# Moving the copy of the scan's last column for two of four channel groups from ScalarE to VectorE, in a state-space network on one core

## The chip, the cores and the metric

The kernel runs on one core of a Trainium2 chip. The metric is the device time in microseconds. Before the change the median of three runs is 6207.15 us (6202.91 to 6214.02).

The core's engines work side by side, each on its own queue in order: TensorE (PE in the profile; PEld is its weight load), VectorE (DVE), ScalarE (ACT), GpSimd (POOL), and SyncE (SP), which only issues DMAs here. An instruction waits on semaphores for what others have to finish first; all behind it on the same engine wait with it.

## What is computed

Input x is 8 images of 384 channels and 32 x 32 pixels. Four layers follow one another, each a group norm, a block, and a residual sum. Layers 0 and 2 are Mamba blocks, and they hold the part that matters here, a recurrence along the 1024 pixels of an image:

```python
def step(h, inp):
    dA_t, dBu_t, C_t = inp          # exp(dt*A), dt*u*B, C
    hst = dA_t * hst + dBu_t
    return (hst, jnp.einsum('bdn,bn->bd', hst, C_t))
```

There are 768 inner channels d with 16 states n each, so 12,288 independent recurrences for each image. Layer 1 is a 1x1 convolution, a filter in the frequency domain of 8 x 8 patches, a 3 x 3 depthwise convolution and a gate; layer 2 has an MLP behind its Mamba block; layer 3 is a 3 x 3 depthwise convolution.

## The kernel before

**Tiling.** An image is cut into two halves of T = 512 pixels (NCH = 2). A half of a layer-0 or layer-2 image is a *chunk*: 2 layers x 8 images x 2 halves = 32 chunks. A chunk has NQ = 24 *steps*; a step is 4 groups (j = 0 to 3) of 128 recurrences (8 channels x 16 states), so 768 steps in all. The chunk's number in its image is `s["c"]`: 0 for the first half, 1 for the second.

**A step t**, with the function that writes each part:

- `begins`: a DMA brings dt*u, repeated over the states, into the SBUF tile `g` (128 x 4 x 512, AHEAD + 1 = 5 buffers).
- `times`: GpSimd multiplies all of g by B (one instruction, 128 x 2048).
- `decays`: TensorE writes dt for each group into its PSUM bank `dA{j}`; the four banks are used by every step.
- `exps`: ScalarE turns each bank into exp(dt*A).
- `scans`: VectorE runs the recurrence of each group as one scan instruction of 512 columns. SHARE is 2 everywhere, so `low` is 2: the scans of groups 0 and 1 write into g (SBUF), those of groups 2 and 3 into their banks (PSUM). Then VectorE multiplies groups 2 and 3 by C, from the banks into g.
- `carries`: in a first half (`s["c"] == 0`) the last column of each scan is kept in the SBUF tile `carry`, since the second half starts from it (line 847). ScalarE does it before the change: one copy of 128 x 2 for groups 0 and 1 together (line 868) and one of 128 x 1 for each bank (line 873). A second half has no such copies.
- `states`: GpSimd multiplies groups 0 and 1 by C, in place in g (one instruction, 128 x 1024). In place means that the last columns must have been copied before: the condition is `carried(t, 0)` (line 886).
- `gathers`: TensorE sums the 16 states of all four groups into `y`, `gatings`: VectorE multiplies y by the gate z.

**Side jobs.** `front` prepares the next chunk (projections, a short convolution, softplus, three-part bf16 copies of dt), `finish` projects the chunk before, and `layer1`, `mlp` and `layer3` run between the steps, all on the same engines.

**Order.** Nothing is scheduled on the chip: each engine executes its list in order. The lists are written ahead by a planner in the kernel, `Order`, which runs the generators above as processes. Each process yields the engine that it wants and a condition; `Clocks.op` keeps an estimate of when each engine is free and each piece of data is known, by prices of its own (a VectorE instruction: 0.075 us plus 0.00104 a column; a GpSimd instruction: 0.14 plus 0.00212 a column). The planner always lets that process go on which can begin first. GpSimd's list is therefore an alternation of `times` for a later step and `states` for an earlier one, with the side jobs' instructions between. TensorE may overwrite a bank for the next step when it has been read (line 816 to 818; for groups 2 and 3 that includes the carry).

All engine calls go through one helper, so nearly every instruction of the profile stands at L189; they are told apart by the tiles that they write and read.

Of the kernel before, what the change touches and what calls it, by code (L numbers as in the profile page):

```python
# [11 lines left out]
AF = mybir.ActivationFunctionType  # L12
# [13 lines left out]
T = 512  # L26
NCH = L // T
# [222 lines left out]
def tile_conv_preact_d4(ctx: ExitStack, tc: tile.TileContext, a: dict, out: bass.AP):  # L250
# [10 lines left out]
    clocks = Clocks()  # L261
    order = Order(clocks)
    tensor = Timed(nc.tensor, clocks, "PE")
    vector = Timed(nc.vector, clocks, "DVE")
# [18 lines left out]
    def on(engine, *aps, when=None, due=None, next_=False):  # L283


        def ready():
            t = when() if when else 0.0
            return None if t is None else max(t, clocks.known(*aps) if aps else 0.0)

        return engine, ready, due, next_  # L290
# [8 lines left out]
    class Tokens:  # L299
# [5 lines left out]
        def when(self):  # L305
            return min(self.free) if self.free else None
# [62 lines left out]
    def exp_set():  # L369
        nc.scalar.preload_act_table_set(SET_EXP)  # L370
        clocks.free["ACT"] += 1.28
        act_set["now"] = "exp"

    def act(out_, in_, func, **kw):
        if func in (AF.Exp, AF.Ln):
            if act_set["now"] != "exp":
                exp_set()
        elif func not in (AF.Identity, AF.Copy, AF.Square, AF.Abs):
            if act_set["now"] != func:
                clocks.free["ACT"] += 1.28  # L380
            act_set["now"] = func
        scalar.activation(out_, in_, func, **kw)
# [28 lines left out]
    carry = const.tile([P, 4 * NQ], F32, name="carry")  # L411
# [355 lines left out]
    said = {}  # L767

    def seen(*keys):


        def ready():
            return None if any(k not in said for k in keys) else 0.0

        return ready
# [57 lines left out]
    def scans():  # L833
        for t, (s, i) in enumerate(steps):
            for j in range(4):
                yield on("DVE", dAs[j], when=lambda: (
                    None if ("exp", t, j) not in said or ("times", t) not in said
                    else clocks.known(s["g", i][:, j, :])
                ))
                g = s["g", i]  # L840
                low = 4 - SHARE[i % NSUB]
                q = 4 * i + j
                vector.tensor_tensor_scan(
                    g[:, j, :] if j < low else dAs[j],
                    dAs[j],
                    g[:, j, :],
                    0.0 if s["c"] == 0 else carry[:, q : q + 1],
                    ALU.mult,
                    ALU.add,
                )  # L850
                ahead["scans"] += 1
                said["scan", t, j] = True
            for j in range(low, 4):
                yield on("DVE", dAs[j])
                vector.tensor_mul(g[:, j, :], dAs[j], s["bc"][:, 1, :])
                said["product", t, j] = True
            start_jobs(t + 1)

    def carries():
        for t, (s, i) in enumerate(steps):  # L860
            if s["c"] == NCH - 1:
                continue
            low = 4 - SHARE[i % NSUB]
            yield on("ACT", when=lambda: (
                None if ("scan", t, low - 1) not in said else clocks.known(s["g", i][:, 0:low, :])
            ))
            g = s["g", i]
            act(carry[:, 4 * i : 4 * i + low].unsqueeze(2), g[:, 0:low, T - 1 : T], AF.Copy)
            said["carry", t, 0] = True
            for j in range(low, 4):  # L870
                q = 4 * i + j
                yield on("ACT", dAs[j], when=seen(("scan", t, j)))
                act(carry[:, q : q + 1], dAs[j][:, T - 1 : T], AF.Copy)
                said["carry", t, j] = True
# [470 lines left out]
    def start_jobs(t):  # L1345
        n, i = divmod(t, NQ)
        if i or n >= len(chunks):
            return
        s = chunks[n]
        order.add(gates(s, 1), t + 8)  # L1350
        if s["c"] == 0 and n + NCH < len(chunks):
            m = chunks[n + NCH]
            order.add(measured(m), t + NQ + 4)
        if n + 1 < len(chunks):
            later = chunks[n + 1]
            order.add(front(later), t + NQ - 26)
            order.add(gates(later, 0), t + NQ - 4)
        order.add(finish(s), t + NQ + 10)
# [28 lines left out]
    for name, gen in (  # L1387
        ("begins", begins), ("times", times), ("decays", decays), ("exps", exps),
        ("scans", scans), ("carries", carries), ("states", states), ("gathers", gathers), ("gatings", gatings),
    ):  # L1390
        p = procs[name] = {
            "gen": gen(), "due": 0, "ready": 0.0, "done": None, "first": ("PE", "ACT", "SP"),
        }
        order.processes.append(p)
        order.advance(p)
# [141 lines left out]
```

## Time and profile before

| | |
|---|---|
| median of three runs | 6207.15 us |
| the profiled execution | 6204.07 us |
| its span, first to last instruction | 6202.2 us |
| granted TensorE clock, mean | 0.973 |
| ScalarE, carry<-g, 128x2 | x384, 205 ns mean, 78.8 us |
| ScalarE, carry<-dA, 128x1 | x768, 174 ns mean, 133.4 us |
| GpSimd, `times` (128x2048) | x768, 4535 ns mean, 3479.6 us |
| GpSimd, `states` (128x1024) | x768, 2359 ns mean, 1810.9 us |
| VectorE, scans without and with a carry | 1209 to 1212 and 1269 to 1271 ns |
| VectorE, product with C (128x512, one operand in PSUM) | x1536, 677 ns mean |
| VectorE, COPY | x1 (gain<-ps_gain, 128x384 out of PSUM) |

How to read it: the profile groups instructions by the tiles that they write and read (`carry<-g` writes carry and reads g), gives their number, the busy time, the mean duration, and the idle time of the engine right before them with what ended it. A share of busy time is an average over chunks of four kinds (first and second halves, layer 0 and layer 2), so a view of one chunk tells more. A chunk of 24 steps takes 169 to 199 us between 1506 and 4928 us.

### The profile page before, as it was taken

What the parts mean: (1) busy time and instruction counts of PE and PEld (TensorE: products, weight loads), DVE (VectorE), ACT (ScalarE), POOL (GpSimd) and SP (SyncE); (2) the same over time, 40 slices, a digit from 0 to 9 for tenths busy, and PEclk for the clock granted to TensorE, in tenths of its full rate; (3) what the DMA queues carried; (4) which work ended last, traced back from release to release, by engine and by line L of the source; (5) the groups of instructions that cost most, each with busy time, mean ns of one, the idle gap of its engine ahead of it and who ended that gap; (6) DMA issues with size and microseconds to landing.
All of it is one profiled execution on the core that took longest, in us unless ns stands there. A gap on an engine that the chain in (4) does not pass through costs nothing.

```text
span 6202.2 us, 62614 instructions
## 1 busy us (share of the span) xinstructions
PE 5799.2 (94%) x19022; PEld 2184.1 (35%) x19022; DVE 5616.8 (91%) x6381; ACT 4241.3 (68%) x7942; POOL 5725.3 (92%) x2028
## 2 busy tenths in 40 slices
PE   6878999999999999999989999999999999999998
PEld 2223333333333333333333333333333333333333
DVE  5999999999998999998887899899998999989994
ACT  5656677677667767776676676777767777677753
POOL 4999999999999999989997999999999999999991
PEclk8889999999999999999999999999999999999999
DMA  6877878877887888787777888878888788888871
GB/s 178 193 184 186 195 190 194 204 188 193 190 193 185 196 205 189 192 205 186 180 185 183 199 196 219 200 198 209 198 215 201 200 207 198 212 205 197 207 197 58
DMA packets 346724, 1195.88 MB, mean 193 GB/s; under 512 B 40516, under 2 KB 142580, under 8 KB 248084
## 3 DMA queue, kind: packets, MB, share of 16 engines
q1 hardware_dynamic: 346388, 1191.88, 79.1%
q8 instruction: 152, 2.49, 0.2%
q14 instruction: 184, 1.51, 0.1%
HBM read 1040.73 MB, written 150.99 MB: 192 GB/s over the span
## 4 chain that ended last, share of the span: by engine, by line
DVE 25%; PE 13%; POOL 8%; DMA 4%; issue 4%; ACT 4%; SPq 0%; POOLq 0%; DVEq 0%; ACTq 0%
DVE g L189 11%; DVE dA L189 8%; POOL g L189 6%; DVE u L189 2%; PE ps_dn L189 2%; PE ps_up L189 2%; PE ps_dw L189 2%; PE y L189 2%; PE dA L189 2%; DMA g<-dud 2%; DVE ps_dw L189 1%; PE ps_z L189 1%; DMA dts<-dtd 1%; PE ps_out L189 1%; DVE st L189 1%
## 5 line engine op out<-in xcount | busy, mean ns | idle before, releaser
L189 POOL TENSOR_TENSOR g<-g,bc 128x1024 f32<-128x1024 f32 (+1 forms) x1536 | 5243.4, 3447 | 248.1 <-ACT carry L189 94.1
L189 ACT ACTIVATE dA<-dA,w_A 128x512 f32<-128x512 f32 x3072 | 2018.6, 661 | 931.0 <-PE dA L189 919.4
L189 PE MATMUL dA<-dts,selr 96*128 96x512 bf16 x3072 | 1190.0, 390 | 233.2 <-DVE g L189 207.6
L189 DVE TENSOR_TENSOR_SCAN g<-dA,carry,g 128x512 f32<-128x512 f32 x768 | 955.4, 1269 | 75.1 <-POOL g L189 61.1
L189 DVE TENSOR_TENSOR g<-dA,bc 128x512 f32<-128x512 f32 x1536 | 994.5, 677 | 17.3 <-ACT carry L189 16.4
L189 DVE TENSOR_TENSOR_SCAN g<-dA,g 128x512 f32<-128x512 f32 x768 | 909.4, 1209 | 85.7 <-POOL g L189 77.8
L189 DVE TENSOR_TENSOR_SCAN dA<-dA,carry,g 128x512 f32<-128x512 f32 x768 | 952.2, 1271 | 28.0 <-ACT dA L189 27.4
L189 DVE TENSOR_TENSOR_SCAN dA<-dA,g 128x512 f32<-128x512 f32 x768 | 909.0, 1212 | 62.3 <-ACT dA L189 61.7
L189 PE MATMUL y<-g,sely 128*32 128x512 f32 x6144 | 857.0, 627 | 38.0 <-POOL g L189 35.6
L189 PEld LDWEIGHTS <-selr 96*128 96x128 bf16 x3072 | 300.2, 98 | 1113.0 <-issue 1072.0
L189 PE MATMUL ps_in<-xf,w_in 128*128 128x512 f32 x1152 | 562.7, 610 | 10.0 <-ACT xf L189 7.6
L189 PE MATMUL ps_z<-xf,w_z 128*128 128x512 f32 x1152 | 567.8, 597 | 3.6 <-DVE dt L189 3.6
L189 PE MATMUL ps_up<-t,mw 128*128 128x512 f32 x1152 | 556.0, 596 | 7.1 <-DVE u L189 5.2
L189 PE MATMUL ps_out<-u,w_out 128*128 128x512 f32 x1152 | 547.5, 594 | 0.4 <-ACT carry L189 0.4
L189 PE MATMUL ps_dn<-h,mw 128*128 128x512 f32 x1152 | 545.3, 594 | 1.6 <-ACT h L189 1.6
L189 PE MATMUL ps_dw<-tp,diag 128*128 128x512 f32 x864 | 438.8, 609 | 9.6 <-ACT diag L189 9.6
L189 PEld LDWEIGHTS y<-g,sely 128*32 128x32 f32 x6144 | 126.3, 109 | 599.2 <-issue 313.0
L189 PEld LDWEIGHTS ps_in<-xf,w_in 128*128 128x128 f32 x1152 | 218.6, 195 | 263.8 <-issue 234.2
L189 POOL TENSOR_TENSOR dt<-dt,u 128x512 f32<-128x512 f32 x192 | 244.3, 1274 | 72.4 <-PE ps_dr L189 56.3
L189 PEld LDWEIGHTS ps_dn<-h,mw 128*128 128x128 f32 x1152 | 217.8, 190 | 259.9 <-issue 235.3
L189 PEld LDWEIGHTS ps_up<-t,mw 128*128 128x128 f32 x1152 | 214.4, 190 | 267.2 <-issue 230.4
L189 PEld LDWEIGHTS ps_z<-xf,w_z 128*128 128x128 f32 x1152 | 215.9, 191 | 252.7 <-issue 215.2
(118 smaller groups left out, 6451.1 us busy)
## 6 DMA issues: line engine op xcount, KB each, us to landing
g<-dud SPq DMA_DIRECT2D x768, 1024.0 KB, 8.2
dtd<-pc SPq DMA_DIRECT2D x192, 384.0 KB, 4.0
dts<-dtd SPq DMA_DIRECT2D x192, 384.0 KB, 7.8
mw<-in_l_mlp_w SPq DMA_DIRECT2D x192, 384.0 KB, 6.5
dud<-dt SPq DMA_DIRECT2D x768, 64.0 KB, 3.2
xf<-in_x SPq DMA_DIRECT2D x16, 768.0 KB, 9.1
x<-in_x SPq DMA_DIRECT2D x16, 768.0 KB, 11.9
x_mid<-x SPq DMA_DIRECT2D x16, 768.0 KB, 7.0
```

The source lines that it names most:

```text
L189: return call(out_, *args, **kw)
```

## The change

VectorE copies the last columns of groups 0 and 1 itself, in one instruction that stands right behind the scan of group 1 and ahead of the scan of group 2. It is no process of its own: it is written in the same turn of `scans` as that scan. ScalarE keeps the copies of the two banks. The condition of `states`, `carried(t, 0)`, is the same and is now met by VectorE.

```diff
@@ scans
                 ahead["scans"] += 1
                 said["scan", t, j] = True
+                if j == low - 1 and s["c"] < NCH - 1:
+                    vector.tensor_copy(
+                        carry[:, 4 * i : 4 * i + low].unsqueeze(2), g[:, 0:low, T - 1 : T]
+                    )
+                    said["carry", t, 0] = True
             for j in range(low, 4):
@@ carries
             low = 4 - SHARE[i % NSUB]
-            yield on("ACT", when=lambda: (
-                None if ("scan", t, low - 1) not in said else clocks.known(s["g", i][:, 0:low, :])
-            ))
-            g = s["g", i]
-            act(carry[:, 4 * i : 4 * i + low].unsqueeze(2), g[:, 0:low, T - 1 : T], AF.Copy)
-            said["carry", t, 0] = True
             for j in range(low, 4):
```

## The prediction

> **What bounds the kernel now.** I read the page's shares first, then the busy time of the engines in four stretches, one chunk of 24 steps each: a first half and a second half of a layer-0 image, then the same of a layer-2 image.
>
> ```profile
> PE 5799.2 (94%) x19022; PEld 2184.1 (35%) x19022; DVE 5616.8 (91%) x6381; ACT 4241.3 (68%) x7942; POOL 5725.3 (92%) x2028
> ```
> ```profile
> 1506.00:1696.00 190.00, 172.70 (x604) 65.47 (x603) 173.25 (x205) 137.20 (x297) 176.82 (x63) 0.96 0.79 190
> 1696.00:1865.00 169.00, 164.20 (x560) 61.78 (x558) 164.65 (x181) 116.21 (x211) 168.34 (x54) 1.00 0.82 196
> 4542.00:4729.00 187.00, 182.72 (x599) 69.19 (x599) 175.21 (x202) 137.40 (x267) 182.32 (x71) 1.00 0.86 206
> 4729.00:4928.00 199.00, 193.41 (x618) 73.20 (x617) 187.88 (x213) 137.78 (x220) 187.21 (x68) 1.00 0.82 202
> ```
>
> Columns of the second view: stretch, its length, then PE, weight loads, DVE, ACT, POOL, clock, DMA share, GB/s. Only first halves carry anything over, so only they change. There a step takes 190/24 = 7.92 us in layer 0 with VectorE busy 7.22 and GpSimd 7.37, and 7.79 us in layer 2 with VectorE 7.30, GpSimd 7.60 and TensorE 7.61. No engine has 0.8 us to spare except ScalarE (5.7 of 7.9). In a second half of layer 0, without carries, GpSimd is busy 168.3 of 169 us. So VectorE and GpSimd are both near their limit, and the gap between 7.92 and 7.37 is what waits cost. One of these waits is the change's target:
>
> ```profile
> POOL g L189 <- ACT carry L189: 94.1, 54, 7.1
> ```
>
> 54 waits, 94.1 us: GpSimd may not overwrite g with the C product before ScalarE has copied the last column of g, and ScalarE comes to that copy late.
>
> **The change, part by part.**
>
> (a) Removed: 384 ScalarE copies (16 first halves x 24 steps) of 128x2.
>
> ```profile
> L189 ACT ACTIVATE carry<-g 128x2 f32<-128x2 f32 x384 | 78.8, 205 | 43.9 <-DVE g L189 29.7 <-issue 8.3 <-POOL g L189 2.5
> ```
>
> 384 x 0.205 = 79 us less on an engine that is busy 68%. Nothing on the path follows its busy time, so I cost this at nothing by itself. What may follow is the 94.1 us above. Late next would be the scan itself: "POOL g <- DVE g" already stands at 60.2 us. The upper bound of the gain is 94 us.
>
> (b) Added: 384 VectorE copies of 128x2 from SBUF to SBUF, each right behind the scan that wrote its second column. VectorE has no such row. Its smallest: the 128x96 TENSOR_SCALAR at 24.80 us took 0.12 from its start to the next start, and BATCH_NORM_AGGREGATE 0.225 start to start. A dependent pair costs more than an independent one: in layer 2 the gating (u from y) starts 0.034 us behind the end of the instruction that writes its y (96 times), while independent neighbours overlap by 0.084. That is 0.12 us for the wait on the scan. So a copy costs between 0.12 (no bubble) and 0.35 (bubble and the dearer row); I take 0.12 + 0.12 = 0.24, since a copy resembles the plain elementwise row more than the aggregate. 384 x 0.24 = 92 us on VectorE, of which its idle time in first halves (0.65 us a step) could hide most.
>
> (c) The wait that the copy may bring. VectorE's instructions here are nearly all of a kind: one operand in PSUM, one in SBUF. The only plain one-source elementwise instruction from SBUF to SBUF is the scaling of w_A, and there are two of it:
>
> ```profile
> 24.80 0.20 DVE L189 TENSOR_SCALAR w_A<-w_A 128x96 f32<-128x96 f32 x1
> 24.92 0.75 DVE L189 SCALAR_TENSOR_TENSOR u<-ps_in,w_vec,u 128x510 f32<-128x510 f32 x1
> ```
> ```profile
> 2787.11 0.95 DVE L189 TENSOR_SCALAR w_A<-w_A 128x96 f32<-128x96 f32 x1
> 2787.98 1.28 DVE L189 TENSOR_TENSOR_SCAN dA<-dA,carry,g 128x512 f32<-128x512 f32 x1
> ```
> ```profile
> 2783.49 4.51 POOL L189 TENSOR_TENSOR g<-g,bc 128x2048 f32<-128x2048 f32 x1
> ```
>
> The columns are start, duration, engine. At 24.8 us GpSimd runs nothing and the instruction takes 0.20 us. At 2787 the same instruction takes 0.95, and it ends at 2788.06, 0.06 behind the end of GpSimd's 4.51 us product (2783.49 + 4.51 = 2788.00). I read this as VectorE held until GpSimd's running instruction is done. Against it stands a one-source SBUF row that is not stretched, BATCH_NORM_STATS2 (676 ns mean over 96 calls), so not every such instruction is held; the copy resembles the scaling more than the statistics.
>
> [...]
>
> What would the hold cost? I took the end of the second scan in each of the 384 first-half steps and looked at what GpSimd was running. In 332 of them it was inside an instruction, mostly the 4.5 us one. One such step:
>
> ```profile
> 1624.76 2.33 DVE L189 TENSOR_TENSOR_SCAN g<-dA,g 128x512 f32<-128x512 f32 x2
> 1627.00 2.32 DVE L189 TENSOR_TENSOR_SCAN dA<-dA,g 128x512 f32<-128x512 f32 x2
> ```
> ```profile
> 1626.16 4.52 POOL L189 TENSOR_TENSOR g<-g,bc 128x2048 f32<-128x2048 f32 x1 [1.58 <-DMA g<-dud]
> ```
>
> Now the second pair of scans starts at 1627.00. With the copy ahead of them they would wait until GpSimd is done at 1630.68, 3.6 us later. Summed over the 384 steps the rest of GpSimd's instruction is 711 us, 1.85 a step. Queued behind the copy on VectorE are the two scans in PSUM, both products, the next step's scans, and the convolutions and sums of the side jobs; exps, PSUM banks, TensorE's next decays and GpSimd's next C product wait for these.
>
> 711 us will not all show. Once VectorE is late, GpSimd runs out of work at the C product of that step (it needs the scan and the copy), stands idle, and the copy passes at once. The hold thus turns two loosely coupled queues into two that meet once a step, at the end of a GpSimd instruction. A step then takes about the longer of VectorE's work from copy to copy and GpSimd's work from C product to C product. I added both up per first-half step in the trace (all but the first chunk, which is start-up), with 0.24 us for the copy, and averaged the larger of the two: 8.22 us in layer 0 against 7.91 now, 8.49 in layer 2 against 7.82. That is 0.31 x 192 + 0.67 x 192 = 60 + 129 = 188 us. Busy times hold no waits, so the removed 94 us is already inside this difference. The order is written anew by the planner, which knows no hold; a more even alternation would lower the sum, waits on TensorE and DMAs would raise it.
>
> (d) Nothing else moves: no DMA, no semaphore on SP, and TensorE's condition for the next decays asks only for the copies from the two banks, which stay.
>
> **Sum.** 6204.07 us (the profiled execution: span 6202.2 and 1.9 around it; 0.05% under the median of 6207.15) + 188 = 6392, say 6390, 3.0% slower.
>
> **Rivals.**
> 1. *No hold, the change does what its words suggest* (the other side). For it: the statistics row, and that 2 elements are very few. Against it: the 0.95 us row. Then GpSimd gets back its 94 us and VectorE gives 92, about half of it hidden: 6204 - 94 + 46 = 6156, with ends at 6110 (all hidden) and 6202 (none hidden). It decides from the point where a copy takes under about 0.5 us with GpSimd busy.
> 2. *The hold in full.* VectorE does not settle behind GpSimd but asks at any moment, as now: 711 + 92, less its present idle time of 0.65 x 384 = 250, gives 553: 6757. For it: 270 of the 332 cases fall into the 4.5 us instruction, and VectorE is as busy as GpSimd. Against it: GpSimd then idles ahead of each C product and lets the copy through.
> 3. *The hold is there but hidden.* VectorE settles so that nearly every copy finds GpSimd waiting for it; only (a) and (b) are left, 6204 - 94 + 92 = 6202. In the trace only 52 of 384 moments are like that.
>
> **How the numbers follow.** Forecast 0.55, rival 1 0.20, rival 2 0.15, rival 3 0.10. Changes under 0.2% can't be told from none. Rival 1 gives 0.16 faster, 0.03 same, 0.01 slower; rival 3 gives 0.02, 0.06, 0.02; forecast and rival 2 are slower. So 0.18, 0.09, 0.73. The forecast alone spans 6270 to 6550 (half and nearly twice its sum). For 8 in 10 the range takes in rival 3, the upper half of rival 1 and the lower part of rival 2: 6150 to 6650.
>
> **What would show it.** A row of VectorE copies, x384: a mean of 1 to 2 us, ending with GpSimd's instructions, shows the hold; 0.1 to 0.3 us refutes it. ScalarE's carry<-g row and GpSimd's waits on ACT carry for g should go in every case. First halves should go from 7.8-7.9 to 8.2-8.5 us a step, second halves stay at 7.05 and 8.3; GpSimd's idle time should end on VectorE. If copies are long but steps are not, rival 3 holds; a copy mean near 1.9 and steps over 9 us mean rival 2. The prediction is wrong if two elements do not count as that kind of instruction.

## The result, and the profile after

| | before | after |
|---|---|---|
| median of all runs | 6207.89 us (6202.91 to 6214.02, 4 runs) | 6510.57 us (6507.76 to 6520.41, 4 runs) |
| profiled execution | 6204.07 us | 6512.05 us |
| its span | 6202.2 us | 6510.2 us |

The ratio is 1.0492, with a 95% interval of 1.0479 to 1.0505: slower by 4.9%. The forecast was slower by 3.0% (6390 us), the range 6150 to 6650.

The shares of the profile after, to be set beside those of before:

```profile
PE 5886.7 (90%) x19022; PEld 2212.6 (34%) x19022; DVE 6015.9 (92%) x6765; ACT 4196.9 (64%) x7558; POOL 5732.6 (88%) x2028
```

VectorE has 384 instructions and 399 us of busy time more. GpSimd has the same work (5733 against 5725 us) and a smaller share: it waits more. Where the 399 us are, and for what GpSimd waits, two groups tell (columns as on the page: busy us, mean ns, idle time ahead and what ended it):

```profile
L189 DVE COPY carry<-g 128x2 f32<-128x2 f32 x384 | 402.2, 1047 | 13.1
L189 POOL TENSOR_TENSOR g<-g,bc 128x1024 f32<-128x1024 f32 x768 | 1807.8, 2355 | 350.6 <-DVE carry L189 267.8 <-DVE g L189 71.6 <-DMA g<-dud 2.1
```

A copy of two columns takes 1047 ns on average, nearly as long as a scan of 512 (1205 ns). GpSimd's C product, which waited 94 us for ScalarE's copy, now waits 268 us for VectorE's. The stretches of the first halves (chunks 8 and 24, the same as shown of before, and the second half behind each):

```profile
1567.00:1767.00 200.00, 172.17 (x591) 65.78 (x590) 192.60 (x228) 131.51 (x270) 180.39 (x64) 0.96 0.77 183
1767.00:1938.00 171.00, 165.15 (x563) 61.14 (x563) 165.89 (x184) 120.55 (x215) 167.97 (x53) 1.00 0.80 191
4732.00:4943.00 211.00, 189.67 (x600) 71.04 (x600) 206.62 (x225) 133.96 (x242) 184.85 (x73) 0.98 0.77 191
4943.00:5143.00 200.00, 189.18 (x604) 70.95 (x604) 189.43 (x215) 135.61 (x216) 192.96 (x68) 0.97 0.81 197
```

The first halves went from 190 to 200 and from 187 to 211 us, the second halves from 169 to 171 and from 199 to 200. Over all chunks the first halves hold 304 of the 308 us that the span grew by.

How a copy comes to be long is best seen in a row of steps of chunk 24, VectorE first, then GpSimd (start, duration, and in brackets the idle time ahead; a row of x2 or x3 is a run of instructions and shows the shape of its first alone):

```profile
4803.62 4.35 DVE L189 COPY carry<-g 128x2 f32<-128x2 f32 x1
...
4818.69 0.17 DVE L189 COPY carry<-g 128x2 f32<-128x2 f32 x1
...
4826.47 3.87 DVE L189 COPY carry<-g 128x2 f32<-128x2 f32 x1
```
```profile
4801.11 6.83 POOL L189 TENSOR_TENSOR g<-g,bc 128x1024 f32<-128x1024 f32 x2
4808.11 6.82 POOL L189 TENSOR_TENSOR g<-g,bc 128x1024 f32<-128x1024 f32 x2 [0.17 <-DVE carry L189]
4819.00 11.31 POOL L189 TENSOR_TENSOR g<-g,bc 128x1024 f32<-128x1024 f32 x3 [4.08 <-DVE carry L189]
4830.49 6.83 POOL L189 TENSOR_TENSOR g<-g,bc 128x1024 f32<-128x1024 f32 x2 [0.17 <-DVE carry L189]
```

The first copy starts at 4803.62 and ends at 4807.97; GpSimd's pair of products ends at 4801.11 + 6.83 = 4807.94. The third ends at 4830.34, GpSimd's three at 4819.00 + 11.31 = 4830.31. Between them stands a copy of 0.17 us: GpSimd was idle (4.08 us) and waited for it. So either VectorE waits for GpSimd or GpSimd for VectorE, about once a step. Of the 384 copies 219 took over 0.4 us, and 210 of those ended 0.024 to 0.030 us behind the end of a GpSimd instruction; 196 of the 219 began within a 128x2048 one. Behind 137 of the other 165 GpSimd had been waiting for the copy (over 0.15 us), which leaves 28 steps in which neither waited.

### The profile page after: what moved, and what is told of

It reads as the page before. It is cut to its first block, busy times and chain, and to the rows that moved or that the text cites. A ratio compares the mean times of both kernels' runs of the same rounds, so it can differ in the third digit from the quotient of the medians.

```text
span 6510.2 us, 62617 instructions
## 1 busy us (share of the span) xinstructions
PE 5886.7 (90%) x19022; PEld 2212.6 (34%) x19022; DVE 6015.9 (92%) x6765; ACT 4196.9 (64%) x7558; POOL 5732.6 (88%) x2028
## 4 chain that ended last, share of the span: by engine, by line
DVE 37%; PE 17%; ACT 9%; POOL 7%; issue 5%; DMA 2%; SPq 0%; DVEq 0%; POOLq 0%; ACTq 0%
DVE g L189 15%; DVE dA L189 11%; POOL g L189 5%; DVE carry L189 3%; PE ps_dw L189 3%; DVE u L189 3%; PE y L189 3%; PE ps_up L189 2%; PE dA L189 2%; PE ps_dn L189 2%; ACT dA L189 2%; PE ps_z L189 1%; ACT L189 1%; ACT L370 1%; DMA g<-dud 1%
## 5 line engine op out<-in xcount | busy, mean ns | idle before, releaser
L189 POOL TENSOR_TENSOR g<-g,bc 128x2048 f32<-128x2048 f32 (+1 forms) x1536 | 5247.8, 3443 | 436.4 <-DVE carry L189 269.2
L189 PE MATMUL dA<-dts,selr 96*128 96x512 bf16 x3072 | 1205.4, 395 | 404.3 <-DVE g L189 383.5
L189 DVE TENSOR_TENSOR_SCAN g<-dA,g 128x512 f32<-128x512 f32 x768 | 905.1, 1205 | 50.4 <-POOL g L189 36.6
L189 PE MATMUL y<-g,sely 128*32 128x512 f32 x6144 | 874.8, 635 | 32.4 <-POOL g L189 31.4
L189 PE MATMUL ps_dn<-h,mw 128*128 128x512 f32 x1152 | 563.6, 610 | 7.1 <-ACT z L189 5.0
L189 ACT ACTIVATE carry<-dA 128x1 f32<-128x1 f32 x768 | 132.0, 173 | 454.8 <-DVE dA L189 437.3
L189 DVE COPY carry<-g 128x2 f32<-128x2 f32 x384 | 402.2, 1047 | 13.1
```

What stands on the lines that cost most here:

```text
L189: return call(out_, *args, **kw)
```

## The experiments

My theory: VectorE's copy of two SBUF columns to SBUF waits until GpSimd's running instruction ends, as the 210 copies that end 0.024 to 0.030 us behind one do, and a copy of one column does not. Rival A: the loss comes from the place of the copy and the order that the planner made with it. Rival B: any SBUF to SBUF copy, or any copy of two elements, is held. Twelve kernels were run. "Held" is a row over 0.4 us. The diffs show the lines of the step; the declarations of extra tiles are left out.

**Two copies of one column** (`e1_two_singles`). The planner is told the price of the single copy, so each engine's order is that of the changed kernel.

```diff
-                    vector.tensor_copy(
-                        carry[:, 4 * i : 4 * i + low].unsqueeze(2), g[:, 0:low, T - 1 : T]
+                    clocks.op(
+                        "DVE", "tensor_copy", carry[:, 4 * i : 4 * i + low].unsqueeze(2),
+                        [g[:, 0:low, T - 1 : T]],
                     )
+                    for k in range(low):
+                        nc.vector.tensor_copy(
+                            carry[:, 4 * i + k : 4 * i + k + 1], g[:, k, T - 1 : T]
+                        )
```

> The 128x2 copy is cut into two copies of 128x1 at the same place; every engine's order is that of the changed kernel. [...] Rival A (the time comes from where the copy stands and from the order the planner made of it, not from a hold): 6500 to 6560 us, since place and order are the same and one more instruction is added. Rival B (any SBUF to SBUF copy on VectorE is held): at least 6500 us, with rows up to 4.5 us.

Measured: 6231.02 us, ratio to before 1.0044 (1.0030 to 1.0058). None of the 768 copies is held, the longest takes 0.157 us.

```profile
L859 DVE COPY carry<-g 128x1 f32<-128x1 f32 x768 | 104.0, 141 | 0.0
```

Twice the instructions and a quarter of the time. Rival A falls, and with it the first half of rival B: 280 us of the loss go, with the place and the order unchanged.

**The same two columns by a reduction** (`e2_reduce`).

```diff
-                    vector.tensor_copy(
-                        carry[:, 4 * i : 4 * i + low].unsqueeze(2), g[:, 0:low, T - 1 : T]
+                    vector.reduce_max(
+                        carry[:, 4 * i : 4 * i + low], g[:, 0:low, T - 1 : T], axis=mybir.AxisListType.X
                     )
```

> The copy is written as a maximum over one element (a reduction of 128x2x1 to 128x2): the same data, count, place and order as in the changed kernel, another operation. Theory (the hold belongs to copies and their like, as the batch-norm statistics row suggests it is not every one-source SBUF instruction): rows of 0.1 to 0.3 us, 6150 to 6220 us. Rival A (place and order): 6500 to 6530. Rival B (any one-source SBUF to SBUF instruction of two elements is held): 6500 to 6530, rows up to 4.5 us.

Measured: 6225.02 us, ratio 1.0036 (1.0023 to 1.0049).

```profile
L189 DVE TENSOR_REDUCE carry<-g 128x2 f32<-128x2 f32 x384 | 59.6, 155 | 13.2
```
```profile
POOL g L189 <- DVE carry L189: 123.4, 72, 5.6
```

The first line is VectorE's group, the second GpSimd's wait (total, times, longest). This is the cleanest pair of the study: one operation swapped, all else the same, 6511 - 6225 = 286 us. TensorE's granted clock, 0.973 before and 0.959 after, is 0.970 here, so its fall went with the hold; no run sets the clock alone. The run also shows what rival 1 had wrong: without any hold the change is still no gain, but 0.36% slower. The 94 us that GpSimd waited for ScalarE became 123 us that it waits for VectorE. I had expected up to 6220 here, and it came out a little above.

**A copy that nobody needs** (`e3_dummy_pair` and `e4_dummy_single`). The kernel before, ScalarE's copies left in, and an unused copy between constant tiles added; in the second run one column, in the same order. The planner's order is not that of the kernel before.

```diff
+                if j == low - 1 and s["c"] < NCH - 1:
+                    clocks.op("DVE", "tensor_copy", spare2, [vec2[:, 0:2]])
+                    nc.vector.tensor_copy(spare2[:, 0:2], vec2[:, 0:2])
```

> The kernel before, with ScalarE's carry copies left as they are, and a copy of 128x2 from one constant SBUF tile to an unread one added behind the second scan of each first-half step. Nothing waits for it but what stands behind it on VectorE. Theory (hold): 384 copies of about 1 to 1.8 us mean, 6207 plus 150 to 450 = 6360 to 6660 us. Rival A (the loss comes from the carry's dependency on VectorE and GpSimd's wait for it): 6207 plus 0 to 60, copies of 0.1 to 0.3 us.

> The same with a copy of 128x1 in place of 128x2; every engine's order is that of the run with the 128x2 copy. Theory: no hold, copies of 0.1 to 0.2 us, 6207 plus 0 to 60 us. Rival B (any SBUF copy is held): as the 128x2 copy, within 1%.

Measured: 6602.46 us (1.0642, 1.0628 to 1.0657) with two columns, 6258.12 us (1.0086, 1.0073 to 1.0100) with one. VectorE's groups of the two runs:

```profile
L856 DVE COPY spare<-vec 128x2 f32<-128x2 f32 x384 | 453.2, 1180 | 0.0
```
```profile
L856 DVE COPY spare<-vec 128x1 f32<-128x1 f32 x384 | 48.8, 127 | 0.0
```

One useless column more costs 344 us. No step waits for the copied data and the order is the same, so the hold alone does it. The 54 us that the single column costs beside the kernel before can't be put down to the copies: measured from scan to scan, the first halves, where the copies stand, are 3 us longer in all, and the second halves, which have none, 49 us. The new order has moved 45 us of GpSimd's work into the second halves. What 49 us of unheld VectorE work cost by themselves is thus not shown.

**Shorter GpSimd instructions** (`e5_split_times`, and `e7_split_reduce` with the reduction in the same order). GpSimd's product with B is cut in two.

```diff
-            gpsimd.tensor_mul(g, g, s["bc"][:, 0, :].unsqueeze(1).to_broadcast([P, 4, T]))
+            for h in range(2):
+                gpsimd.tensor_mul(
+                    g[:, 2 * h : 2 * h + 2, :], g[:, 2 * h : 2 * h + 2, :],
+                    s["bc"][:, 0, :].unsqueeze(1).to_broadcast([P, 2, T]),
+                )
```

> The changed kernel with GpSimd's product with B (128x2048) cut into two instructions of 128x1024; the 128x2 copies stay. Theory (a copy is held until GpSimd's running instruction ends): no copy lasts over about 2.6 us (4.48 in the changed kernel), the mean falls from 1.05 to 0.5 to 0.8 us, and the distance to the run with the same cut and the unheld reduction is 120 to 220 us (with uncut products it was 6510 minus 6225 = 285 us). Rival (a held copy waits for something else, a queue or a fixed time that does not follow the length of GpSimd's instruction): mean about 1.05, longest about 4.5, distance about 285 us.

> The same cut with the reduction of 128x2x1 in place of the copy; every engine's order is that of the run before. It gives the floor for the distance. The cut itself adds to GpSimd 768 x (2 x 2.36 - 4.535) = 142 us of work where it is the bound, so 6225 plus 50 to 200 us = 6275 to 6425 us; reductions of 0.15 us, none over 0.4.

Measured: 6512.12 us (1.0493, 1.0477 to 1.0508) and 6269.30 us (1.0098, 1.0083 to 1.0113), the second just under the 6275 to 6425 that I expected. The distance is 243 us, outside my 120 to 220, and the mean of a copy, 1.051 us, did not fall at all. The trace shows why. 218 of the 233 held copies ended with the GpSimd instruction that they began in; their mean fell from 1.69 to 1.30 us and none was over 2.36, the length of one half. That part of the theory holds. But 15 copies did not end with that instruction, and stood through one to four more; they took 92 us together, one of them 10.2. In the changed kernel there was one such copy. The clearest case is in the dummy run `e3_dummy_pair`, where one copy stands through the rest of a GpSimd instruction and three whole ones behind it; VectorE, then GpSimd:

```profile
3173.88 11.73 DVE L856 COPY spare<-vec 128x2 f32<-128x2 f32 x1
```
```profile
3172.03 2.33 POOL L189 TENSOR_TENSOR g<-g,bc 128x1024 f32<-128x1024 f32 x1
...
3174.32 4.50 POOL L189 TENSOR_TENSOR g<-g,bc 128x2048 f32<-128x2048 f32 x1
...
3178.79 2.34 POOL L189 TENSOR_TENSOR g<-g,bc 128x1024 f32<-128x1024 f32 x1
...
3181.09 4.49 POOL L189 TENSOR_TENSOR g<-g,bc 128x2048 f32<-128x2048 f32 x1
...
3196.03 2.36 POOL L189 TENSOR_TENSOR g<-g,bc 128x1024 f32<-128x1024 f32 x1 [10.45 <-ACT carry L189]
```

It ends at 3185.61, 0.03 us behind the fourth one's end at 3185.58. All these instructions follow each other without a gap. In the changed kernel GpSimd mostly has to stop for the copy (its C product needs it): behind 173 of the 219 held copies' GpSimd instructions there is a gap, 0.168 us in the median. But the missing gap alone does not decide: where a held copy met an end with the next GpSimd instruction right behind it, it ended there at 46 of 47 such ends in the changed kernel, at 188 of 197 in `e3_dummy_pair`, and at 80 of 114 in `e5_split_times`. What decides which copies last beyond an end is not settled.

**Two SBUF inputs** (`e8_two_inputs`).

```diff
-                    vector.tensor_copy(
-                        carry[:, 4 * i : 4 * i + low].unsqueeze(2), g[:, 0:low, T - 1 : T]
+                    vector.tensor_add(
+                        carry[:, 4 * i : 4 * i + low].unsqueeze(2), g[:, 0:low, T - 1 : T], none2.unsqueeze(2)
                     )
```

> The carry of the two groups written as a sum of g's last columns and a 128x2 SBUF tile of zeros: two SBUF inputs, 128x2, same place. [...] Theory in its narrow form (only copies and scalings are held): rows of 0.15 to 0.3 us, 6210 to 6260 us.

Measured: 6591.54 us, 1.0619 (1.0598 to 1.0640).

```profile
L189 DVE TENSOR_TENSOR carry<-g,none 128x2 f32<-128x2 f32 x384 | 453.7, 1181 | 13.2
```

Held like the copy, up to 4.54 us, so the narrow form is wrong: a sum of two SBUF inputs, neither a copy nor a scaling, waits too. The time came out far above the narrow form's 6210 to 6260, in another order of the planner's.

**From a bank, and three columns** (`e11_dummy_bank`, `e12_dummy_three`). One execution each, on the dummy; the diff is that of `e12_dummy_three` beside `e3_dummy_pair`.

```diff
-                    nc.vector.tensor_copy(spare2[:, 0:2], vec2[:, 0:2])
+                    nc.vector.tensor_copy(spare3, vec2[:, 0:3])
```

> The kernel before with an unused 128x2 copy as in the dummy run of 128x2, but out of a PSUM bank (two elements of group 1's bank, already read by its scan). [...] Rival (any copy of two elements is held): mean about 1.2 us and about 6600 us.

> The dummy run of 128x2 with three columns, 128x3 to 128x3, every engine's order the same. [...] Rival (only an even count is held): 0.1 to 0.2 us a copy and 6230 to 6290 us.

Measured: 6261.59 us out of the bank (`vector.tensor_copy(spare2, dAs[1][:, 0:2])`, planned as such), 6611.14 us with three columns. VectorE's groups:

```profile
L189 DVE COPY spare<-dA 128x2 f32<-128x2 f32 x384 | 52.5, 137 | 0.0
```
```profile
L857 DVE COPY spare<-vec 128x3 f32<-128x3 f32 x384 | 458.8, 1195 | 0.0
```

Two columns out of PSUM are not held (137 ns), three out of SBUF are (1195 ns), like two (1180 ns). Both rivals fall, and with the first of them the second half of rival B.

**Versions that might beat both.** All four carries on VectorE as single columns (`e6_all_vector`): the scan of group 3 is followed by two copies out of the banks, and `carries` is gone.

> All four carries on VectorE, each as a 128x1 copy: two from g behind the second scan, two from the banks behind the fourth; ScalarE copies none. No copy is held by the theory. VectorE gains 768 copies out of PSUM of about 0.15 us (115 us in all) in first halves where it is nearly full; ScalarE loses 768 x 0.174 = 133 us that it does not need. Expected 6230 to 6330 us; under 6204 only if the 12.6 us that TensorE and the 16 us that VectorE wait for ScalarE's bank copies stand for more than they show.

Measured: 6299.07 us, 1.0143 (1.0126 to 1.0160). The 768 copies out of the banks take 0.154 us each, none is held.

GpSimd copies for itself (`e9_gpsimd_copies`; VectorE's copy in `scans` is gone, and the C product waits for the scan alone):

```diff
+            if s["c"] < NCH - 1:
+                gpsimd.tensor_copy(
+                    carry[:, 4 * i : 4 * i + low].unsqueeze(2), s["g", i][:, 0:low, T - 1 : T]
+                )
+                said["carry", t, 0] = True
```

> GpSimd copies the 128x2 carry itself, directly ahead of its product with C; neither ScalarE nor VectorE has a part in it. If the 94 us that GpSimd waited for ScalarE's copy were to be had by leaving ScalarE out, less 384 GpSimd copies of 0.1 to 0.2 us (40 to 77 us): 6150 to 6190 us. If that wait only stood in front of the scan's own lateness (the unheld reduction on VectorE left 123 us of GpSimd waiting on it, and its wait for the scan alone at 64): 6200 to 6260 us, and GpSimd's wait ends on VectorE's scan of g.

Measured: 6250.13 us, 1.0063 (1.0051 to 1.0076). GpSimd's waits:

```profile
POOL carry L189 <- DVE g L189: 74.9, 33, 6.4
...
POOL g L189 <- DVE g L189: 42.5, 24, 6.0
```

With no other engine between scan and product, GpSimd still waits 75 us for the scan at its own copy, and the copies cost it 71 us. The second reading is right: a good part of the 94 us was never ScalarE's.

The reduction in layer 0 only (`e10_layer0_only`):

> The unheld reduction on VectorE in layer 0 only; in layer 2 ScalarE copies as before. In the run with the reduction in both layers a first-half step took 7.83 us in layer 0 (7.88 before) and 7.96 in layer 2 (7.81 before). If these differences hold one by one: 6204 - 0.05 x 192 = 6180 to 6205 us. If they are the planner's luck with one order: 6205 to 6240 us.

Measured: 6228.93 us, 1.0032 (1.0021 to 1.0043). The gain of the first halves did carry over: they are 8.5 us shorter in all than before, near the 10 us hoped for. But the second halves, which copy nothing, are 33 us longer in the order that the planner made anew. The kernel before stays the fastest of all that were run.

## Why the prediction was right, point by point

**(a) The removed ScalarE copies** were costed at nothing for ScalarE and at most 94 us for GpSimd's wait. No gain was seen. Counted by what ended it, GpSimd's wait moved from "ACT carry" (94 us) to "DVE carry" (123 us in `e2_reduce`). Held against the ends of the scans in the trace, the 94 us of before fall into 48 that passed before the second scan was done, and 46 behind it; only the 46 were ScalarE's. In `e2_reduce` 102 of the 123 us lie ahead of the scan's end and 22 behind it. So what could be had was 46 - 22 = 24 us, against 384 x 0.19 = 73 us on VectorE, and the sum came to +21. The order of `e2_reduce` is not that of before, so the +21 is not taken apart further. I had read the 94 us as one thing, because the wait view names only what came last.

**(b) The added copy** was put at 0.24 us. Where it is not held it adds 0.195 from the scan to the next instruction: 0.034 + 0.084 for the wait on the scan, as taken from the gating pair, and 0.077 for the copy, where I had taken 0.12. The row of 96 columns was too dear for two. Whether VectorE's idle time hides most of it stays open: the 54 us of `e4_dummy_single` lie in the second halves, where the order differs and no copy stands.

**(c) The hold** was the step that decided, and it is shown. The one row at 2787 us in the trace of before told it: 0.95 against 0.20 us, ending with GpSimd. In the trace after the same scaling starts at 2919.40 and takes 3.04 us; it ends 0.07 us behind GpSimd's product (2917.86 + 4.51 = 2922.37). That a copy of two columns would wait like this scaling, and not pass like the statistics, was my estimate by likeness; `e1`, `e2` and the dummies confirm it at 280, 286 and 344 us. Between SBUF tiles, a copy of two columns is held (mean 1047 ns), so is one of three (1195 ns), and so is a sum of two SBUF inputs (1181 ns). A single column is not (141 ns in `e1_two_singles`, 127 in `e4_dummy_single`), nor is a reduction (155 ns), nor a copy of two columns out of PSUM (137 ns). What makes VectorE wait, no run shows. The statistics row (676 ns), which spoke against a hold, is no copy; the reduction of `e2_reduce`, no copy either, is not held.

**The size** was the weak point: +188 forecast, +303 by the medians. The forecast took a step as the longer of VectorE's and GpSimd's work, 8.22 and 8.49 us. Measured are 8.43 us in layer 0 (without the first chunk) and 8.82 in layer 2. VectorE's busy time, holds included, is 8.07 and 8.40, near the forecast. The term that was missing is VectorE's idle time, 0.36 and 0.41 us a step, which the forecast let vanish: 0.36 x 192 + 0.41 x 192 = 148 us. The forecast lay 0.15 and 0.09 above the busy time, 46 us, so 102 us of the 115 that it fell short are told. I had named waits on TensorE and DMAs and priced them at nothing. The largest part is for ScalarE (0.21 and 0.22 us a step), then GpSimd (0.05 and 0.10) and TensorE (0.06 and 0.07); for DMAs VectorE waited next to nothing. The prediction's span of 6270 to 6550 is also wider than its words: half of the 188 us, added to 6204, is 6298.

**That the two queues meet once a step** is what the rows at 4803 to 4830 us show. The forecast's sum, done again from copy to copy on the trace after without the holds, gives 8.05 and 8.54 us a step. In `e2_reduce`, with the same order and no hold, the steps run below such a sum (7.85 and 8.01 against 8.04 and 8.52), since the queues can run ahead of each other; with the hold they lie above it (8.45 and 8.83). The holds add up to 402 - 384 x 0.17 = 337 us, half of the 711 that the full rest of GpSimd's instructions would have made (rival 2: 6757 us). With rival 2 the 711 would have stayed.

**Rival 1** (no hold, 6156 us) was wrong twice: the hold is there, and without it the kernel takes 6225, not 6156, outside even its own ends (6110 to 6202). Half of the gain that it counted was not there to be had (see (a)). **Rival 3** (hold hidden, 6202 us) is refuted by the 219 copies that were held and by the time: GpSimd's 268 us of waits would have suited it, but not the 337 us of holds.

## What to carry to other kernels

Where GpSimd runs long instructions back to back (2.4 and 4.5 us here), look at each VectorE instruction that adds two SBUF tiles (1181 ns for 128x2 in `e8_two_inputs`) or copies more than one column from SBUF to SBUF (1047 ns for two): 219 of the 384 copies of two columns lasted here to the end of a GpSimd instruction, and what stood behind them in the queue waited too (behind the 11.73 us copy of `e3_dummy_pair`, from 3173.88 us, the next scan starts at 3185.52). Single columns (141 ns), a reduction (155 ns) and a copy out of PSUM (137 ns) were not held here; write it as one of these. And a wait that the profile puts down to a small helper instruction is worth removing only if what comes in front of the helper is done long before; here the scan was next, and most of the wait stayed. Two kernels whose lists the planner orders anew differ by tens of us in places that the edit does not touch (33 and 49 us in the second halves of `e10_layer0_only` and `e4_dummy_single`); an effect of that size needs a pair with the same order.

## What the runs showed of the hardware that I had not expected

- A held copy did not always end with the GpSimd instruction that it began in. With gapless GpSimd instructions it stood through the rest of one and up to four whole ones: 10.2 us in `e5_split_times`, and through up to three in `e3_dummy_pair` (11.73 us) and `e12_dummy_three` (11.74 us). That is why halving GpSimd's instructions did not lower the mean (1.051 against 1.047 us).
- From two to three columns the hold stays the same: 128x2 and 128x3 take 1.180 and 1.195 us in the same order, and a single column, not held, 0.127.
- GpSimd's instructions did not get longer in return: its 128x2048 product took 4531 ns after and 4535 before.
